# Layer 0 of a four-layer network: the up product of a group of rows in seven block products, relu and square on ScalarE, and two buffers for drawn weights

## The chip, the cores and the metric

The kernel runs on one core of a Trainium2 chip. The time is device microseconds of one execution of the whole program; the number given for a kernel is the median of its runs. Besides the timed runs there is one profiled execution, from which every duration below comes.

A core has five engines that the profile names: PE (TensorE, the matrix array), DVE (VectorE), ACT (ScalarE), POOL (GpSimd) and SP (SyncE, which here mainly issues DMAs). PEld is PE's loading of the stationary operand. They run their own instruction streams in order and wait for each other by semaphores. SBUF is the on-chip memory; PSUM takes the results of PE; this kernel uses it as eight banks of 128 by 512 float32.

## The reference

Four layers follow each other on x, 64 sequences of 32 rows, 512 wide (2048 rows in all), all in float32. Only layer 0 matters here:

```
w = weight[ids]                            # one of 8 drawn 512x512 matrices per sequence
y = einsum('bsi,boi->bso', x, w)
logits = y @ gate_w                        # 8 experts; the sum of the two largest is r
h = relu(y @ up_w) ** 2                    # 512 -> 1024
shared_out = h @ down_w                    # 1024 -> 512
routed_out = (((y @ fc1_w) @ expert_w) * r) @ fc2_w
x = x + layernorm(shared_out + routed_out) * gamma + beta
```

`y` and the product `y @ up_w` are the parts that the change touches. Layers 1 to 3 (layer 1 gated with low-rank adapters, layer 2 attention with a cache, layer 3 a drawn small product, each with a feed-forward part) stay as they are.

## The kernel before, in words

**Tiling.** `layer0` (L133) cuts the 2048 rows into 16 tiles of 128 rows, and the tiles into 4 groups of 4 tiles (N = 512 rows). A tile holds 4 sequences. Feature dimensions are cut into chunks of 128: 4 for the width 512, 8 for the 1024 features.

**The drawn product.** All 8 matrices lie in SBUF (`sets`). One `step` (L204 to L214) makes a quarter of one tile's `y`: it copies, for each of the 4 sequences of the tile, the drawn 128x512 block (an address read from a register) into `w`, the first `by` of them on DVE and the others on ACT (L208), and then issues 4 matmuls (L212), each with 32 rows of x as the stationary operand and one block as the moving one. They write four different groups of 32 rows of one bank, and the trace shows them beside each other. `w` comes from the pool `sp` with 3 buffers, handed out in turn: the copies of a step wait until PE has read the buffer that it takes over.

**Order of the work.** `on_pe` chains every matmul of the layer to the one issued before it, so PE runs in the order in which the program lists them. The other engines' orders are set by a scheduler, which keeps each engine's instructions in order of need.

1. Opening phase: 32 steps form `y` of groups 0 and 1 in 8 banks (k outermost, then 8 tiles), with `by` 3 and 2 in turn. `y` is then copied out of PSUM (`copied`, L242, and `second`, L253) and transposed (`turned`, L216 to L221: four PE transposes and an ACT copy into `yT`).
2. Group 0: for each of 8 chunks f, `features` (L266) makes 512 rows of one chunk: 4 matmuls of 128x512 into one bank `ph` (L225), ACT's relu from it into `hT` (L273), and DVE's multiplication of that with `ph` again (L274), which is relu squared. Beside the first four, `latent_rows` (L258) forms fc1 · expert.
3. Then tile after tile, in `Tile`: `choose` (the router and the latent product `pl`, top-2 sum, `routed`), `shared` in two halves (8 matmuls of `down` into `pd`), `turn` (two transposes into `eT`), `last` (fc2 on top of `pd`, then layernorm: DVE statistics, a power on POOL, DVE's `z` at L315, POOL's multiplication with gamma at L316 and addition of beta at L317, DVE's final addition at L318, and the store).
4. The steps for groups 2 and 3 (`products`, 16 per group, all 4 copies on DVE) are mixed as stretches into the features loops of groups 1 and 2: after each of the 7 remaining chunks 2 or 3 steps. Their `y` is transposed in the tile loop. The first chunk of the next group's features comes ahead of the last tile's `last`.

**PSUM.** Banks by tag: `tr` twice (transposes, `pl`, `latent_rows`), `mm` twice (`ph`, `pd`), and `y0` to `y3` for the four accumulators of `products`. The opening phase uses all eight for its eight tiles.

**Loads.** SP issues the loads in program order: ids; per k the x of groups 0 and 1 and the 8 blocks of `sets`; `up` in 8 pieces; `fc1T` and `expert`; gate; `down`; fc2; gamma and beta.

Of the kernel before, what the change touches and what calls it, by code (L numbers as in the profile page):

```python
# [36 lines left out]
SEQ = P // S  # L37
KC = D // P
# [94 lines left out]
def layer0(c, x_in, x_out):  # L133
# [4 lines left out]
    tc, nc, a = c.tc, c.nc, c.a  # L138
    INT, LAT, NE = 1024, 256, 8
    G = 4  # L140
    N = G * P
    n_sets = a["cond0T"].shape[0]
    with ExitStack() as ctx:

        fp = ctx.enter_context(tc.tile_pool(name="l0_first", bufs=1))
        sp = ctx.enter_context(tc.tile_pool(name="l0_seq_weights", bufs=3))
        tx = ctx.enter_context(tc.tile_pool(name="l0_transposed_x", bufs=2))
        up_p = ctx.enter_context(tc.tile_pool(name="l0_up", bufs=1))
        wp = ctx.enter_context(tc.tile_pool(name="l0_weights", bufs=1))
# [46 lines left out]
        def sets_of(g, *engines):  # L196

            _, ids = nc.values_load_multi_w_load_instructions(
                numbers[0:1, SEQ * G * g:SEQ * G * (g + 1)], engines=engines,
                min_val=0, max_val=n_sets - 1,  # L200
                skip_runtime_bounds_check_because="numbers holds them between the bounds")
            return ids

        def step(py, xT, ids, t, k, by):  # L204

            w = sp.tile([P, SEQ, D], F32, name="w")
            for j in range(SEQ):
                (nc.vector.tensor_copy if j < by else nc.scalar.copy)(  # L208
                    w[:, j, :], sets[:, k, ds(ids[SEQ * t + j], 1), :].rearrange("p a o -> p (a o)"))
            for j in range(SEQ):  # L210
                q = slice(S * j, S * j + S)
                c.on_pe(nc.tensor.matmul(  # L212
                    py[q, :], xT[:, k, t * P + S * j:t * P + S * j + S], w[:, j, :],
                    start=k == 0, stop=k == KC - 1))  # L214

        def turned(yT, t, y):  # L216

            pt = ps.tile([P, KC, P], F32, tag="tr", name="transposed")
            for k in range(KC):
                c.on_pe(nc.tensor.transpose(pt[:, k, :], y[:, k * P:(k + 1) * P], c.ident))  # L220
            nc.scalar.copy(yT[:, :, t * P:(t + 1) * P], pt)  # L221

        def part(out, pairs, first, last):
            for i, (lhsT, rhs) in enumerate(pairs):
                c.on_pe(nc.tensor.matmul(out, lhsT, rhs, start=first and i == 0,  # L225
                                         stop=last and i == len(pairs) - 1))

        def accumulators():
            return [ps.tile([P, D], F32, tag=f"y{t}", bufs=1, name="py") for t in range(G)]

        def products(g, xT):

            ids, pys = sets_of(g, mybir.EngineType.DVE), accumulators()
            for k in range(KC):
                for t in range(G):
                    step(pys[t], xT, ids, t, k, SEQ)
                    yield pys

        def copied(py, t):

            y = tp.tile([P, D], F32, name="y")
            (nc.scalar.copy if t % 2 else nc.vector.tensor_copy)(y, py)  # L242
            return y

        ids = [sets_of(g, mybir.EngineType.DVE, mybir.EngineType.Activation) for g in range(2)]
        pys = accumulators() + [ps.tile([P, D], F32, tag=("tr", "mm")[t // 2], name="py") for t in range(G)]
        for k in range(KC):
            for t in range(2 * G):
                step(pys[t], xTs[t // G], ids[t // G], t % G, k, 3 - t % 2)
        yTs = [gp.tile([P, KC, N], F32, name="yT") for _ in range(2)]  # L250
        second = gp.tile([P, INT // P, N], F32, name="second", tag="hT", bufs=1)
        for n in range(G):
            (nc.vector.tensor_copy if n % 2 else nc.scalar.copy)(second[:, n, :], pys[G + n])  # L253
        for t in range(G):
            turned(yTs[0], t, copied(pys[t], t))
        for t in range(G):
            turned(yTs[1], t, second[:, t, :])

        def latent_rows(m):
            pl = ps.tile([P, LAT], F32, tag="tr", name="pfe")  # L260
            part(pl, [(fc1T[:, k, m * P:(m + 1) * P], expert[:, k, :]) for k in range(LAT // P)], True, True)
            nc.scalar.copy(latent[:, m, :LAT], pl)

        hTs = {}

        def features(g, f):  # L266

            if f == 0:
                hTs[g] = gp.tile([P, INT // P, N], F32, name="hT", tag="hT", bufs=1)
            ph = ps.tile([P, N], F32, tag="mm", name="ph")  # L270
            part(ph, [(up[:, k, f * P:(f + 1) * P], yTs[g][:, k, :]) for k in range(KC)], True, True)
            h = hTs[g][:, f, :]
            nc.scalar.activation(h, ph, AF.Relu)  # L273
            nc.vector.tensor_tensor(h, h, ph, ALU.mult)  # L274

        class Tile:
            def __init__(self, T):
                self.T, self.g = T, T // G
                self.q = slice(T % G * P, (T % G + 1) * P)

            def choose(self):
                self.xt = c.load(xp, "xt", [P, D], x_in(self.T))
                pl = ps.tile([P, LAT + NE], F32, tag="tr", name="pl")
                part(pl, [(yTs[self.g][:, k, self.q], latent[:, k, :]) for k in range(KC)], True, True)
                top = tp.tile([P, 8], F32, name="top")
                nc.vector.max(top, pl[:, LAT:])
                r = tp.tile([P, 1], F32, name="routed_by")
                nc.vector.tensor_tensor(r, top[:, 0:1], top[:, 1:2], ALU.add)
                self.routed = tp.tile([P, LAT], F32, name="routed")
                nc.scalar.activation(self.routed, pl[:, :LAT], AF.Copy, scale=r)  # L290

            def shared(self, fs):
                if 0 in fs:
                    self.pd = ps.tile([P, D], F32, tag="mm", name="pd")
# [31 lines left out]
        done = {0: KC}  # L326
        for g in range(groups):
            xT = transposed_x(g + 1, None) if 0 < g < groups - 1 else None
            more = iter(()) if xT is None else products(g + 1, xT)
            for f in range(done.get(g, 0), INT // P):  # L330
                features(g, f)
                for _ in range(3 if f in (1, 4) else 2):
                    pys = next(more, None)
            tiles[G * g].choose()
            if xT is not None:
                yTs.append(gp.tile([P, KC, N], F32, name="yT"))
            for t in range(G):
                tile_ = tiles[G * g + t]
                tile_.shared(range(INT // P // 2))
                if xT is not None:  # L340
                    turned(yTs[g + 1], t, copied(pys[t], t))
                tile_.shared(range(INT // P // 2, INT // P))
# [1162 lines left out]
class Tail:  # L1505
# [3 lines left out]
    NE, R = 8, 16  # L1509
# [327 lines left out]
```

## Time and profile before

| | us |
|---|---|
| median of 3 runs | 3500.65 (3500.22 to 3505.04) |
| the profiled execution, its own time | 3498.47 |
| its span, first to last instruction | 3496.7 |
| granted PE clock, mean | 0.997 of full speed |
| layer 0 on PE, first to last matmul | 12.4 to 368.8 |
| opening phase on PE | 12.41 to 43.41 |
| first chunk of features | 49.54 |

| group of instructions of layer 0 | mean ns of one |
|---|---|
| L212 PE py, 128x32 by 128x512 | 613 |
| L225 PE ph, 128x128 by 128x512 | 597 |
| L208 DVE copy into w, 128x512 | 419 |
| L208 ACT copy into w, 128x512 | 617 |
| L273 ACT relu from PSUM, 128x512 | 598 |
| L274 DVE multiplication with PSUM, 128x512 | 687 |
| L303 ACT copy from PSUM, 128x256 | 373 |
| L318 DVE addition in SBUF, 128x512 | 691 |

A line of a group says: source line, engine, operation, result <- operands, shape, and count; then busy time with the mean of one, and the idle time just before with what ended it. A matmul's record is longer than its share of PE's time, since matmuls overlap: the share is read from starts of neighbours in the timeline. Each of these float32 matmuls has two records in the trace, which the text calls passes. In the windows, PEclk is the granted clock as a share of full speed, and DMA share the mean busy share of the 16 DMA engines.

### The profile page before, as it was taken

To read this page: it belongs to the slowest core of one execution; us is meant where nothing else is said; L and a number is where in the kernel's file an instruction comes from. 1 tells how busy PE (TensorE), PEld (TensorE's weight loads), DVE (VectorE), ACT (ScalarE), POOL (GpSimd) and SP (SyncE) were. 2 spreads that over 40 slices of the span, in tenths; PEclk is the share of its full clock that TensorE was granted. 3 is DMA by queue.
4 is the path that set the end of the run, shared out by engine and by line. 5 is a ranking of instruction groups with operands and counts; after the bars stand their busy time and mean duration, and the time that the engine had idled before them with its cause. 6 is when DMAs were issued, how large, how long until landed. Compare 5 with 4: busy or idle time off the path is not lost. (4 is left out here: it accounts for less than half of the span.)

```text
span 3496.7 us, 65764 instructions
## 1 busy us (share of the span) xinstructions
PE 3432.7 (98%) x20736; PEld 2601.2 (74%) x20736; DVE 2124.5 (61%) x5284; ACT 1554.7 (44%) x4089; POOL 1617.2 (46%) x1606
## 2 busy tenths in 40 slices
PE   8999999999999999999999999999999999999999
PEld 4445788888856778777787787777877778778755
DVE  4443534434457676766767767677676676766433
ACT  4111222222226555655555555555565555555411
POOL 0112432323336645645556455465564655644232
PEclk9999999999999999999999999999999999999999
DMA  6013454544466788888878888878888788887721
GB/s 220 25 34 126 159 168 154 168 151 157 139 202 213 239 261 251 259 258 256 257 249 258 255 250 258 262 251 267 256 260 262 247 267 250 259 259 241 228 85 58
DMA packets 630635, 736.00 MB, mean 210 GB/s; under 512 B 64274, under 2 KB 480018, under 8 KB 630290
## 3 DMA queue, kind: packets, MB, share of 16 engines
q1 hardware_dynamic: 577810, 558.74, 51.4%
q0 software_dynamic: 50176, 168.86, 13.9%
q8 instruction: 168, 2.75, 0.3%
q10 hardware_dynamic: 2304, 4.20, 0.3%
q14 instruction: 177, 1.45, 0.1%
HBM read 689.61 MB, written 41.94 MB: 209 GB/s over the span
## 5 line engine op out<-in xcount | busy, mean ns | idle before, releaser
L957 POOL DMA_INDIRECT vt<-in_v_rows,v_rows x512 | 512.5, 1001 | 304.9 <-PE po L931 178.7
L1220 ACT ACTIVATE pr<-pr,low 128x544 f32<-128x544 f32 x512 | 383.3, 749 | 532.3 <-DVE low L1218 486.0
L1213 PE MATMUL sc<-kt,qT 128*128 128x288 f32 (+1 forms) x2048 | 555.5, 394 | 8.1 <-DVE low L1218 6.5
L931 PE MATMUL po<-prT,vt 128*128 128x128 f32 x4096 | 544.9, 276 | 7.4 <-ACT prT L1231 5.9
L931 PEld LDWEIGHTS po<-prT,vt 128*128 128x128 f32 x4096 | 522.7, 192 | 39.1 <-ACT prT L1231 19.0
L1213 PEld LDWEIGHTS sc<-kt,qT 128*128 128x128 f32 x2048 | 385.1, 190 | 223.1 <-issue 123.0
L1218 DVE CUSTOM_DVE_ANT_0 pr<-sc,mask 128x544 f32<-128x544 f32 x512 | 368.2, 719 | 139.3 <-PE sc L1213 101.5
L1005 POOL TENSOR_TENSOR projected<-projected,swapped 128x512 f32<-128x512 f32 x160 | 208.4, 1302 | 300.9 <-DVE projected L1004 277.8
L1225 DVE TENSOR_SCALAR pr<-pr,low 128x512 f32<-128x512 f32 x512 | 315.3, 616 | 12.8
L926 PE MATMUL prT_ps<-ident,pr 128*128 128x128 f32 x2048 | 311.7, 275 | 2.6 <-DVE pr L1225 2.4
L1231 ACT COPY prT<-prT_ps 128x512 f32<-128x512 f32 x512 | 294.0, 574 | 35.2 <-PE prT_ps L926 20.1
L1222 DVE RECIPROCAL low<-low 128x1 f32<-128x1 f32 x512 | 82.0, 160 | 312.8 <-ACT pr L1220 245.7
L926 PEld LDWEIGHTS prT_ps<-ident,pr 128*128 128x128 f32 x2048 | 237.4, 142 | 11.8 <-issue 3.8
L931 PE MATMUL py<-wo,oT 128*128 128x256 f32 x1024 | 241.8, 379 | 0.0
L931 PE MATMUL pq<-wp,x_sums 128*128 128x512 f32 x512 | 240.8, 593 | 0.9 <-issue 0.5
L931 PEld LDWEIGHTS py<-wo,oT 128*128 128x128 f32 x1024 | 186.5, 190 | 21.1
L130 POOL TENSOR_TENSOR rs<-rs,minus_half 128x4 f32<-128x4 f32 x160 | 181.0, 1131 | 22.5 <-DVE low L1222 14.9
L931 PE MATMUL pq<-wp,xT 128*128 128x512 f32 x384 | 182.0, 597 | 3.9 <-DVE projected L1091 3.9
L931 PE MATMUL py<-wo,o_sum 128*128 128x256 f32 x768 | 181.4, 380 | 4.4 <-DVE o_sum L1149 2.5
L1223 ACT ACTIVATE own_pr<-pr,low 128x32 f32<-128x32 f32 x512 | 164.9, 322 | 46.2 <-DVE low L1222 37.4
L1006 POOL TENSOR_TENSOR projected<-projected,rs 128x512 f32<-128x512 f32 x160 | 172.4, 1078 | 7.9
L964 ACT COPY own_vt<-v 32x128 f32<-32x128 f32 x512 | 150.8, 295 | 54.9 <-PE po L931 42.4
(283 smaller groups left out, 6197.7 us busy)
## 6 DMA issues: line engine op xcount, KB each, us to landing
kt<-in_kT SPq DMA_DIRECT2D x2048, 64.0 KB
wp<-in_sums SPq DMA_DIRECT2D x192, 512.0 KB
wo<-out_sums SPq DMA_DIRECT2D x128, 512.0 KB
wp<-in_WqT SPq DMA_DIRECT2D x96, 512.0 KB
wo<-in_WoT SPq DMA_DIRECT2D x96, 512.0 KB
down1T<-in_down1T SPq DMA_DIRECT2D x80, 256.0 KB
wp<-in_WkT SPq DMA_DIRECT2D x32, 512.0 KB
xt<-x SPq DMA_DIRECT2D x48, 256.0 KB
```

The source lines that it names most:

```text
L130: self.nc.gpsimd.tensor_tensor(t, t, self.minus_half[:, :n], ALU.pow)
L926: c.on_pe(nc.tensor.transpose(pt[:, m, :], piece, c.ident))
L931: c.on_pe(nc.tensor.matmul(out, lhsT, rhs, start=first and i == 0, stop=last and i == len(pairs) - 1))
L957: nc.gpsimd.indirect_dma_start(out=vts[b % 2][:, n, :], out_offset=None, in_=a["v_rows"], in_offset=bass.IndirectOffsetOnAxis(ap=rows[h][: ...
L1005: nc.gpsimd.tensor_tensor(src, src, tmp, ALU.add)
L1006: nc.gpsimd.tensor_tensor(src, src, rs.unsqueeze(2).to_broadcast([P, REP, HD]), ALU.mult)
L1213: c.on_pe(nc.tensor.matmul(sc[:, lo + n * PSIZE:lo + m * PSIZE].rearrange("p (n k) -> p n k", k=PSIZE), q, kt[:, n:m, g, :], start=True, s ...
L1218: nc.vector.tensor_tensor_reduce(pr[:, :NK], sc[:, lo:lo + NK], masks[h, b], -SCALE, 3.0e38, ALU.add, ALU.min, low[:, 0:1])
L1220: nc.scalar.activation(pr[:, :NK], pr[:, :NK], AF.Exp, bias=low[:, 0:1], scale=-1.0, accum_out=low[:, 1:2])
L1223: nc.scalar.activation(own_prs[b % 2][:, g * S:(g + 1) * S], pr[:, L:NK], AF.Copy, scale=low[:, 2:3])
L1225: nc.vector.tensor_scalar(pr[:, :L], pr[:, :L], low[:, 2:3], None, ALU.mult)
L1231: last_prT.append(nc.scalar.copy(prT, pt).ins)
```

## The change

1. **The up product of a group.** yT (512 features by 512 rows) and `up` (512 by 1024) are treated as 2x2 blocks for each pair of chunks (f, f + 4): two halves of the contraction, two halves of the rows, and the two chunks. The class `Up` forms the four result blocks from seven block products (the Strassen-Winograd scheme) instead of eight; each product is 2 matmuls of 128x256 (`block`). The sums of `up` (`up_sums`, four DVE subtractions per pair) are made once, the sums of `yT` (`sums`, four DVE operations of 128x512) once per group. Three PSUM banks collect: a takes products 1, 6, 7; b takes 2 in its first half and 4 in its second; c takes 5 and 3. ACT copies the intermediate values v1, v5, v6, v7 out of PSUM, and four DVE additions make the result blocks in `hT`: L309 after product 2, L311 after 3, L314 after 7, L316 after 4.
2. **relu and square** are two ACT instructions for each chunk (L319, L320), on SBUF. DVE no longer multiplies.
3. **Order.** In group 0 the products run 1, 2, 5, 6, 3, 7, 4; in the others 1, 5, 6, 3, 7, 2, 4, with two steps of `products` after 5 and two after 7: eight stretches of two, where there were seven. Products 1 and 5 of the next group go ahead of the last tile's `last`.
4. **`products`** copies 3 blocks on DVE and 1 on ACT.
5. **Buffers.** `w` has two buffers instead of three. `fc1T` and `expert` are loaded into buffers of the tags `z` and `xt`. PSUM tags are single banks: tr, a, b, c, y0 to y3. `pl` goes to a, `pd` to c and b in turn, and the transposes after the opening phase alternate between tr and c.

The core of the diff:

```diff
-        sp = ctx.enter_context(tc.tile_pool(name="l0_seq_weights", bufs=3))
+        sp = ctx.enter_context(tc.tile_pool(name="l0_seq_weights", bufs=2))
...
-        ps = ctx.enter_context(tc.tile_pool(name="l0_psum", bufs=2, space=PSUM))
+        ps = ctx.enter_context(tc.tile_pool(name="l0_psum", bufs=1, space=PSUM))
...
-        fc1T = c.chunks(fp, "fc1T_0")
-        expert = c.chunks(fp, "expert0")
+        fc1T = [c.load(tp, "fc1T", [P, D], a["fc1T_0"][k * P:(k + 1) * P, :], tag="z") for k in range(LAT // P)]
+        expert = c.load(xp, "expert", [P, LAT // P, LAT], a["expert0"].rearrange("(k p) n -> p k n", p=P), tag="xt")
...
-                    step(pys[t], xT, ids, t, k, SEQ)
+                    step(pys[t], xT, ids, t, k, SEQ - 1)
...
+        def up_sums(f):
+
+            v11, v12, v21, v22, t1, t2, t3 = (v[:, :, f * P:(f + 1) * P] for v in
+                                              (b11, b12, b21, b22, t_up[:, 0], t_up[:, 1], t_up[:, 2]))
+            nc.vector.tensor_tensor(t1, v12, v11, ALU.subtract)
+            nc.vector.tensor_tensor(t3, v22, v12, ALU.subtract)
+            nc.vector.tensor_tensor(t2, v22, t1, ALU.subtract)
+            nc.vector.tensor_tensor(v12, v21, t2, ALU.subtract)
...
+                nc.vector.tensor_tensor(s1, x21, x22, ALU.add)
+                nc.vector.tensor_tensor(s2, s1, x11, ALU.subtract)
+                nc.vector.tensor_tensor(s3, x11, x21, ALU.subtract)
+                nc.vector.tensor_tensor(s4, x12, s2, ALU.subtract)
+                self.x = {1: x11, 2: x12, 3: s4, 4: x22, 5: s1, 6: s2, 7: s3}
...
+                out = {2: self.b[:, :H], 4: self.b[:, H:]}[m] if m in (2, 4) else self.c if m in (3, 5) else self.a
+                block(out, w, self.x[m], m in (1, 2, 5))
+                if m == 1:
+                    self.v1 = self.kept("v1", out)
+                elif m == 5:
+                    self.v5 = self.kept("v5", out)
+                elif m == 6:
+                    self.v6 = self.kept("v6", out)
+                elif m == 2:
+                    nc.vector.tensor_tensor(h[0][:, :H], out, self.v1, ALU.add)
+                elif m == 3:
+                    nc.vector.tensor_tensor(h[1][:, :H], out, self.v6, ALU.add)
+                elif m == 7:
+                    self.v7 = self.kept("v7", out)
+                    nc.vector.tensor_tensor(h[1][:, H:], out, self.v5, ALU.add)
+                elif m == 4:
+                    nc.vector.tensor_tensor(h[0][:, H:], out, self.v7, ALU.add)
+                if self.done % 7 == 0:
+                    for v in (h[1], h[0]):
+                        nc.scalar.activation(v, v, AF.Relu)
+                        nc.scalar.activation(v, v, AF.Square)
...
-            ph = ps.tile([P, N], F32, tag="mm", name="ph")
-            part(ph, [(up[:, k, f * P:(f + 1) * P], yTs[g][:, k, :]) for k in range(KC)], True, True)
-            h = hTs[g][:, f, :]
-            nc.scalar.activation(h, ph, AF.Relu)
-            nc.vector.tensor_tensor(h, h, ph, ALU.mult)
...
-        for m in range(KC):
-            features(0, m)
-            latent_rows(m)
+        first, order = (1, 2, 5, 6, 3, 7, 4), (1, 5, 6, 3, 7, 2, 4)
+        for f in range(FH):
+            if f + 1 < FH:
+                up_sums(f + 1)
+            for m in first:
+                ups[0].p(f, m)
+            latent_rows(f)
...
-            for f in range(done.get(g, 0), INT // P):
-                features(g, f)
-                for _ in range(3 if f in (1, 4) else 2):
-                    pys = next(more, None)
+            for i in range(ups[g].done, FH * 7):
+                if i % 7 in (2, 5):
+                    for _ in range(2):
+                        pys = next(more, None)
+                ups[g].p(i // 7, order[i % 7])
...
-                    features(g + 1, 0)
-                    done[g + 1] = 1
+                    for m in order[:2]:
+                        ups[g + 1].p(0, m)
```

Line numbers of added lines in the text are those of the changed kernel: the matmuls of the block products are L230, the sums of `up` L261 to L264, the sums of `yT` L276 to L279, the copies v L284.

More of the change, by code (lines that the diff above doesn't have):

```diff
@@ L214, in step, with turned @@
                     start=k == 0, stop=k == KC - 1))
-        def turned(yT, t, y):
-            pt = ps.tile([P, KC, P], F32, tag="tr", name="transposed")
+        def turned(yT, t, y, tag="tr"):
+            pt = ps.tile([P, KC, P], F32, tag=tag, name="transposed")
             for k in range(KC):
@@ L226, in part, with block @@
                                          stop=last and i == len(pairs) - 1))
+        def block(out, w, x, first):
+            for k in range(K2):
+                c.on_pe(nc.tensor.matmul(out, w[:, k, :], x[:, k, :], start=first and k == 0, stop=k == K2 - 1,
+                                         skip_group_check=not first))
         def accumulators():
-            return [ps.tile([P, D], F32, tag=f"y{t}", bufs=1, name="py") for t in range(G)]
+            return [ps.tile([P, D], F32, tag=f"y{t}", name="py") for t in range(G)]
         def products(g, xT):
-            ids, pys = sets_of(g, mybir.EngineType.DVE), accumulators()
+            ids = sets_of(g, mybir.EngineType.DVE, mybir.EngineType.Activation)
+            pys = accumulators()
             for k in range(KC):
                 for t in range(G):
-                    step(pys[t], xT, ids, t, k, SEQ)
+                    step(pys[t], xT, ids, t, k, SEQ - 1)
                     yield pys
@@ L243, in copied @@
             return y
+        K2, H, FH = KC // 2, N // 2, INT // P // 2
+        hTs = {}
+        b11, b12, b21, b22 = [up[:, k * K2:(k + 1) * K2, n * D:(n + 1) * D] for k in range(2) for n in range(2)]
+        t_up = up_p.tile([P, 3, K2, D], F32, name="up_sums")
+        blocks = {1: b11, 2: b21, 3: b22, 4: b12, 5: t_up[:, 0], 6: t_up[:, 1], 7: t_up[:, 2]}
+        def up_sums(f):
[5 more added lines that the diff above has]
+            nc.vector.tensor_tensor(v12, v21, t2, ALU.subtract)
@@ new lines, in layer0, with __init__, sums, kept @@
+        class Up:
+            def __init__(self, g):
+                self.g, self.done = g, 0
+            def sums(self):
+                x11, x12, x21, x22 = [yTs[self.g][:, k * K2:(k + 1) * K2, t * H:(t + 1) * H]
+                                      for t in range(2) for k in range(2)]
+                s = tx.tile([P, 4, K2, H], F32, name="y_sums", tag="xT")
+                s1, s2, s3, s4 = [s[:, i] for i in range(4)]
+                nc.vector.tensor_tensor(s1, x21, x22, ALU.add)
[3 more added lines that the diff above has]
+                self.x = {1: x11, 2: x12, 3: s4, 4: x22, 5: s1, 6: s2, 7: s3}
+            def kept(self, name, src):
+                t = tp.tile([P, H], F32, name=name, bufs=1)
+                nc.scalar.copy(t, src)
+                return t
+            def p(self, f, m):
+                if self.done == 0:
+                    hTs[self.g] = gp.tile([P, INT // P, N], F32, name="hT", tag="hT", bufs=1)
+                self.done += 1
+                h = [hTs[self.g][:, f + FH * n, :] for n in range(2)]
+                w = blocks[m][:, :, f * P:(f + 1) * P]
+                if m == 1:
+                    self.a = ps.tile([P, D], F32, tag="a", name="acc_a")[:, :H]
+                elif m == 2:
+                    self.b = ps.tile([P, D], F32, tag="b", name="acc_b")
+                elif m == 5:
+                    self.c = ps.tile([P, D], F32, tag="c", name="acc_c")[:, :H]
+                out = {2: self.b[:, :H], 4: self.b[:, H:]}[m] if m in (2, 4) else self.c if m in (3, 5) else self.a
+                block(out, w, self.x[m], m in (1, 2, 5))
+                if m == 1:
+                    self.v1 = self.kept("v1", out)
+                elif m == 5:
+                    self.v5 = self.kept("v5", out)
+                elif m == 6:
+                    self.v6 = self.kept("v6", out)
+                elif m == 2:
+                    nc.vector.tensor_tensor(h[0][:, :H], out, self.v1, ALU.add)
[10 more added lines that the diff above has]
+                        nc.scalar.activation(v, v, AF.Square)
@@ L245, in layer0 @@
         ids = [sets_of(g, mybir.EngineType.DVE, mybir.EngineType.Activation) for g in range(2)]
-        pys = accumulators() + [ps.tile([P, D], F32, tag=("tr", "mm")[t // 2], name="py") for t in range(G)]
+        pys = accumulators() + [ps.tile([P, D], F32, tag=("tr", "a", "b", "c")[t], name="py") for t in range(G)]
         for k in range(KC):
@@ L254, in layer0 @@
         for t in range(G):
-            turned(yTs[0], t, copied(pys[t], t))
+            turned(yTs[0], t, copied(pys[t], t), ("tr", "c")[t % 2])
+        ups = [Up(0)]
+        ups[0].sums()
+        up_sums(0)
         for t in range(G):
-            turned(yTs[1], t, second[:, t, :])
+            turned(yTs[1], t, second[:, t, :], ("tr", "c")[t % 2])
         def latent_rows(m):
             pl = ps.tile([P, LAT], F32, tag="tr", name="pfe")
-            part(pl, [(fc1T[:, k, m * P:(m + 1) * P], expert[:, k, :]) for k in range(LAT // P)], True, True)
+            part(pl, [(fc1T[k][:, m * P:(m + 1) * P], expert[:, k, :]) for k in range(LAT // P)], True, True)
             nc.scalar.copy(latent[:, m, :LAT], pl)
[L264 to L269, printed above, removed]
-            ph = ps.tile([P, N], F32, tag="mm", name="ph")
-            part(ph, [(up[:, k, f * P:(f + 1) * P], yTs[g][:, k, :]) for k in range(KC)], True, True)
-            h = hTs[g][:, f, :]
-            nc.scalar.activation(h, ph, AF.Relu)
-            nc.vector.tensor_tensor(h, h, ph, ALU.mult)
         class Tile:
@@ L282, in choose @@
                 self.xt = c.load(xp, "xt", [P, D], x_in(self.T))
-                pl = ps.tile([P, LAT + NE], F32, tag="tr", name="pl")
+                pl = ps.tile([P, LAT + NE], F32, tag="a", name="pl")
                 part(pl, [(yTs[self.g][:, k, self.q], latent[:, k, :]) for k in range(KC)], True, True)
@@ L293, in shared @@
                 if 0 in fs:
-                    self.pd = ps.tile([P, D], F32, tag="mm", name="pd")
+                    self.pd = ps.tile([P, D], F32, tag="cb"[self.T % 2], name="pd")
                 part(self.pd, [(hTs[self.g][:, f, self.q], down[:, f, :]) for f in fs], 0 in fs, False)
@@ L319, in last @@
                 nc.sync.dma_start(x_out(self.T), z)
-        for m in range(KC):
-            features(0, m)
-            latent_rows(m)
+        first, order = (1, 2, 5, 6, 3, 7, 4), (1, 5, 6, 3, 7, 2, 4)
[5 more added lines that the diff above has]
+            latent_rows(f)
         groups = NT // G
         tiles = [Tile(T) for T in range(NT)]
-        done = {0: KC}
         for g in range(groups):
@@ L341, in layer0 @@
                     turned(yTs[g + 1], t, copied(pys[t], t))
+                if t + 1 == G and g + 1 < groups:
+                    ups.append(Up(g + 1))
+                    ups[g + 1].sums()
                 tile_.shared(range(INT // P // 2, INT // P))
```

## The prediction, made before the change was run

> **What bounds the kernel now.** I read four views in this order: the busy table, the waits of TensorE (PE) inside layer 0, the windows, and PE's timeline. The page begins:
>
> ```profile
> span 3496.7 us, 65764 instructions
> PE 3432.7 (98%) x20736; PEld 2601.2 (74%) x20736; DVE 2124.5 (61%) x5284; ACT 1554.7 (44%) x4089; POOL 1617.2 (46%) x1606
> ```
>
> PE is busy for 98% of the span. A time is therefore the sum of what PE does, plus the holes in it. The view of waits for PE, restricted to layer 0 (0 to 370 us), says how few holes there are:
>
> ```profile
> PE py L212 <- DVE w L208: 12.4, 1, 12.4
> PE transposed L220 <- DVE y L242: 1.5, 1, 1.5
> PE pd L225 <- ACT eT L303: 0.5, 1, 0.5
> PE transposed L220 <- ACT yT L221: 0.4, 2, 0.2
> ```
>
> Columns: microseconds in all, number of waits, longest. Apart from the start (12.4) PE waits 2.4 us in 356. Whatever wait the change adds here goes straight into the time. The windows show the opening phase (the 32 steps that form y of groups 0 and 1):
>
> ```profile
> core 0: us, PE busy (x) PEld busy (x) DVE busy (x) ACT busy (x) POOL busy (x), PEclk, DMA share, GB/s
> 20.00:24.00 4.00, 4.00 (x43) 2.77 (x38) 3.98 (x12) 3.83 (x7) 0.00 (x0) 1.00 1.06 388
> 28.00:32.00 4.00, 4.00 (x42) 2.92 (x37) 4.00 (x13) 3.89 (x8) 0.00 (x0) 1.00 1.05 384
> 49.00:370.00 321.00, 319.31 (x1046) 148.62 (x1044) 139.44 (x341) 45.37 (x85) 57.51 (x50) 1.00 0.18 60
> ```
>
> The reader is to see that in this phase PE, VectorE (DVE) and ScalarE (ACT) are all full at once: three engines balanced on one pipeline of copied weights. From 49 us on only PE is full; DVE has more than half of its time free. So the two places must be judged apart. The timeline of PE gives the prices:
>
> ```profile
> 12.41 31.00 PE L212 MATMUL py<-w,xT 128*32 128x512 f32 x256 [12.41 <-DVE w L208]
> 49.54 3.60 PE L225 MATMUL ph<-yT,up 128*128 128x512 f32 x8
> 52.98 1.03 PE L225 MATMUL pfe<-expert,fc1T 128*128 128x256 f32 x4
> 53.84 3.60 PE L225 MATMUL ph<-yT,up 128*128 128x512 f32 x8
> 66.73 13.90 PE L225 MATMUL ph<-yT,up 128*128 128x512 f32 x32
> ...
> 132.47 3.70 PE L225 MATMUL ph<-yT,up 128*128 128x512 f32 x8
> 136.10 1.92 PE L212 MATMUL py<-w,xT 128*32 128x512 f32 x16
> 137.96 3.70 PE L225 MATMUL ph<-yT,up 128*128 128x512 f32 x8
> ```
>
> One feature chunk `ph` (8 records, 512 wide) takes 52.98 − 49.54 = 3.44 us, 3.433 over several, so 0.429 a record. The four 256-wide records of `pfe` take 53.84 − 52.98 = 0.86, so 0.2155 each: half the width costs half. A stretch of two steps takes 137.96 − 136.10 = 1.86 us.
>
> **What is removed.** Two chunks cost 2 × 3.433 = 6.87 us before. Seven block products are 28 records of 256 columns: 7 × 0.862 = 6.03. That is 0.83 us per pair; 4 groups of 4 pairs give **−13.3 us** if PE runs on without holes. Bounds: −13.3, and 0 if a lone product costs more than `pfe` shows. I take −13.3, since `pfe` is the same shape. From the end of the opening phase (43.41) to the first chunk (49.54) stand 6.13 us, with the 1.5 us wait for `y`. In the new order the copies of `y` stand further forward in the queues of DVE and ACT, and the transposes have a second bank as before: bounds 0 and −1.5, taken **−1.0**.
>
> **What is added: the opening phase.** `w` has two buffers instead of three. The first copy of a step waits for PE's last matmul of the step two before, and even and odd steps now keep one buffer each. So one buffer's loop bounds two steps. Its parts are these: three DVE copies, 2 × 0.336 + 0.42 = 1.10 us (or two ACT copies, 0.52 + 0.617 = 1.14); 0.054 from the end of a copy to its matmul; 0.429 for the first pass of that matmul; 0.592 for the last; 0.037 from the matmul's end to the next copy. All are single records of the trace. The sum is 2.21 to 2.25 us. Before, two steps took 1.717, which the third buffer made possible. The rows of these copies, 20 to 40 us:
>
> ```profile
> L208 DVE COPY w<-sets 128x512 f32 x58 | 20.0, 421 | 0.0
> L208 ACT COPY w<-sets 128x512 f32 x35 | 19.4, 617 | 0.6
> ```
>
> 58 copies in 20.0 us are one per 0.345 us without idle time; in the new loop DVE will sit idle. 16 × (2.25 − 1.717) = 8.5; the 0.87 us in which DVE reads the ids of group 1 (16.2 to 17.1 us) no longer has a spare buffer to cover it: **+9.4**. Bounds: 7.9 by the shorter loop without the ids, 10.5 with 2.35 us for copies that queue behind each other and two sums over `up` that now stand between them; and 0 if the loop is covered after all (first rival).
>
> One rule of the Trainium skill speaks against this edit more strongly. Row first: at 384 to 388 us PE is busy for only 1.60 and 1.34 of 2 us, and PEclk stays 1.00.
>
> ```profile
> 384.00:386.00 2.00, 1.60 (x15) 1.41 (x14) 1.00 (x3) 1.74 (x4) 1.33 (x2) 1.00 0.74 228
> 386.00:388.00 2.00, 1.34 (x13) 1.15 (x11) 1.81 (x5) 0.27 (x1) 1.73 (x3) 1.00 0.01 5
> ```
>
> The page "TensorE: Matmul & The Clock Gate", section "A second HAM failure mode: psum-queue depth-cycling", says that frequent short idle times of PE between groups of matmuls can throw the clock back and forth between half and full speed. At half speed throughout, by that rule, the phase would be bound by PE at 3.43 us for two steps and cost about 27 us instead of 9.4. Here PE would be idle for 0.5 us of every 2.2, which is about the share of the rows above, where the clock held. I keep 9.4 and leave a loss of clock to a rival.
>
> **What is added: group 0.** DVE forms the sums over `up` (16 subtractions of 128x256, 0.40 to 0.58 us each by the same subtractions of layer 1) and over `y` (4 of 128x512, 0.69 us each, per group). Most lie beside PE, but when the first pair's adds L311 and L314 fall due, DVE still has the sums of three later chunks and of group 1 ahead, and PE's next p1 waits for its bank: **+1.7** (0 to 3). The first `choose` waits for the last copy into `latent`, which ACT makes after four activations of 0.6 us: **+0.55** (0 to 1.2).
>
> **What is added: the waits in groups 1 to 3.** There is one more stretch per loop in groups 1 and 2. Group 1's loop took 166.24 − 126.23 = 40.0 us by the timeline; less 7 chunks (24.0) and 16 steps of 0.858 (13.7) that leaves 2.3 for the edges of seven stretches, 0.32 each; two more are **+0.64** (0.3 to 1). More important, the order p2, p4 puts two products of one bank next to each other: p4 writes the second half of bank b, and its first matmul waits for DVE's L309, which reads the first half. DVE can begin only when p2 is done. The nearest row is one wait of layer 1, where PE needs a bank that DVE must add from:
>
> ```profile
> 387.90 0.71 PE L450 MATMUL acc_a<-xT,up1T 128*128 128x128 f32 x4 [0.66 <-DVE up L587]
> ```
>
> 0.66 us with an add of 128 columns (0.279 us). An add of 256 columns I estimate at 0.42 from that row and L318's 0.69 for 512. So a bare stall is about 0.7: drain of p2, 0.42, and 0.055 to the matmul. Where three copies for the next stretch are ahead in DVE's queue it is 0.78, at the edges of a group 1.0 to 1.2. Behind p4 stands all of PE. In the first pair of a group DVE also still has `z` of the last tile, whose final add waits for POOL's multiply (1.28 us); behind it wait the copies of the second stretch (0.85 late) and, in group 3, L311 and L314. Group 1: 0.85 + 1.0 + 0.78 + 0.78 + 1.2 = 4.6. Group 2: 0.85 + 1.0 + 0.78 + 0.78 + 0.75 = 4.2. Group 3, without stretches: 0.25 at its first products, 1.9 for the first p4, 3 × 0.7 for the others, 0.3 until `pl` has bank a, 4.5. Together **+13.3** (bounds: 0 if DVE is through in time everywhere; 17 if each stall takes 1.2).
>
> **Costed at nothing.** relu and square: four ACT instructions of 0.6 per pair, against 6 to 9.5 us of PE per pair, and ACT was busy for 45 of 321 us. The four copies v (0.37 each) end before the next product ends that reads their bank. One copy of each step goes from DVE to ACT, one stretch ahead. `fc1T` and `expert` land in other buffers at the same time, before use. If ACT fell behind, p6 and p7 would wait 0.4 each. In group 2's tiles a cosine of a later layer now stands ahead of `eT` on ACT: 0 to 1.5 us, taken 0. Layers 1 to 3 keep their order; the first `xT_ps` still waits for the last `z`.
>
> **Sum.** −13.3 − 1.0 + 9.4 + 1.7 + 0.55 + 0.64 + 13.3 = +11.3. The profiled execution took 3498.47 us (span 3496.7), which gives 3509.8. The median of the runs, 3500.65, is 2.2 above it: **3512 us**.
>
> **Rivals.**
> 1. Two buffers are enough (the other side: not slower). Decides at a loop of 1.72 us per buffer, that is if matmuls of a step release the copies earlier or the copies run at 0.336 without the end. For it: DMA runs at 384 GB/s through the phase and `up` lands only by 38.6, so something else may have set it. Against it: `up` is there 11 us before use, and DVE is at 4.00 of 4. Price −9.4: 3502.5.
> 2. The stalls at p4 hide: DVE has 181 of 321 us free. But a stall is a chain and not a share. If they vanish, the time falls by about 10 (12 stalls): 3502.
> 3. Both: the products bring what they promise, 3512 − 9.4 − 10 = 3492.6, faster by 0.23%.
> 4. More waits than I count: PE's clock falls in the opening phase (it was half until 17.3 us in this trace, with records of 1.06 us for 0.61), or DVE's queue lets every stall reach 1.2 us, and the cosine falls due: +4 to +18, 3516 to 3530; I put 3522.
>
> That the products don't do what they say would be 28 records taking more than 6.87 us together; then only the losses remain, 3525, which I count into the fourth.
>
> **Chances.** Forecast 0.58 (its own range 3507 to 3517), rival 1 0.10, rival 2 0.13, rival 3 0.05, rival 4 0.14. A change under 0.2% (7 us: 3493.7 to 3507.7) is about what a measurement of this kernel can't tell from none. Faster 0.05 (rival 3); same 0.23 (rivals 1 and 2); slower 0.72. The range reaches from rivals 1 and 2 (3502, less 2 for the bounds of the smaller terms) to the lower part of rival 4: 3500 to 3520.
>
> **What would show it.** In the new profile PE's opening phase should end near 53 us with waits on copies L208 of about 0.5 per two steps, and DVE idle there; a phase end at 44 proves rival 1. Four 256-wide records should keep 0.86 us. The view of waits should name L309 as PE's releaser some 12 times at about 0.8; if it is absent, rival 2 holds. PEclk below 1.00 between 20 and 50 us would be rival 4. A shift after layer 0 would prove me wrong about the later layers.

## The result, and the profile after

The changed kernel took **3511.34 us** (median of 15 runs, 3506.12 to 3514.26). Beside it the kernel before took 3503.73 us (15 runs, 3497.21 to 3507.43). The ratio is 1.0024 with a 95% interval of 1.0016 to 1.0032: slower by 6 to 11 us. The profiled execution has a span of 3508.5 us, 11.8 above that of before. 3512 had been forecast from a first median of 3500.65; with more runs that median is 3503.73, so the closeness of the two absolute times is partly luck. The measured rise, 7.6 us between medians, is to be held against a forecast of +11.3.

The profile tells where. The stages of layer 0, from the starts of PE's records:

| stage of layer 0 (us) | before | changed | difference |
|---|---|---|---|
| start to the first up product | 49.54 | 56.24 | +6.70 |
| group 0, up product to its first `pl` | 30.92 | 27.63 | −3.29 |
| from there to the last tile's fc2 product | 286.38 | 292.73 | +6.35 |
| sum | 366.84 | 376.60 | +9.76 |

From layer 1 on the two traces stay 9.4 to 12.3 us apart. Those later 2 us are within what the later layers differ between single profiles (from layer 1's first product `low_ps` to the end, 3112 to 3127 us in the fourteen profiles of this study, except the one with a new wait at the start of layer 1), so only layer 0 is read to a microsecond.

The waits of PE in layer 0 of the changed kernel (microseconds in all, number, longest):

```profile
PE py L212 <- DVE w L208: 12.1, 1, 12.1
PE acc_b L230 <- DVE hT L309: 8.8, 12, 1.6
PE xT_ps L561 <- issue: 2.8, 1, 2.8
```

The second line is new: 12 waits at product 4, one for each pair of groups 1 to 3. But nothing in this view speaks of the opening phase, although it has become 7 us longer. Its windows, the line of PE's timeline, and three groups of 20 to 40 us:

```profile
20.00:24.00 4.00, 4.00 (x32) 1.40 (x26) 3.44 (x10) 3.25 (x6) 0.00 (x0) 1.00 1.05 387
28.00:32.00 4.00, 4.00 (x32) 1.44 (x29) 2.98 (x10) 3.12 (x6) 0.00 (x0) 1.00 1.05 384
```

```profile
12.05 38.43 PE L212 MATMUL py<-w,xT 128*32 128x512 f32 x256 [12.05 <-DVE w L208]
```

```profile
L208 DVE COPY w<-sets 128x512 f32 x45 | 15.9, 422 | 4.3 <-PE py L212 3.7 <-DMA sets<-in_cond0T 0.5
L208 ACT COPY w<-sets 128x512 f32 x27 | 15.9, 619 | 4.7 <-PE py L212 4.7
L212 PEld LDWEIGHTS py<-w,xT 128*32 128x32 f32 x141 | 7.4, 108 | 12.9 <-DVE w L208 12.2
```

PE is still "busy" for 4.00 of 4 us, since the matmuls of the four sequences overlap and a record counts as busy while it lasts. The count in brackets gives it away: 32 records instead of 42 or 43. So do DVE and ACT, which now sit idle for 4.3 and 4.7 of 20 us, 3.7 and 4.7 of that behind PE's release of a buffer, and PEld, which waits 12.2 us for DVE's copies. Each of them waits for another, in a loop through the two buffers. PEclk stays at 1.00.

Two stretches of the timeline show the second loss, in group 1 and in group 3:

```profile
145.32 1.92 PE L212 MATMUL py<-w,xT 128*32 128x512 f32 x16
147.18 1.13 PE L230 MATMUL acc_b<-yT,up 128*128 128x256 f32 x4
148.95 1.13 PE L230 MATMUL acc_b<-yT,up 128*128 128x256 f32 x4 [0.64 <-DVE hT L309]
149.92 1.03 PE L230 MATMUL acc_a<-yT,up 128*128 128x256 f32 x4
...
311.12 1.13 PE L230 MATMUL acc_b<-yT,up 128*128 128x256 f32 x4
313.86 1.13 PE L230 MATMUL acc_b<-yT,up 128*128 128x256 f32 x4 [1.61 <-DVE hT L309]
```

A product should take 0.86 us from start to start. Product 2 at 147.18 takes 1.77, that is 0.91 more: 0.64 in which PE is idle (in brackets), and the rest while its last records still run. Product 4 itself takes 0.97, 0.11 more than a product that follows another without a wait.

### The profile page after: what moved, and what is told of

Its sections match the earlier page's. It is cut to its first block, busy times and chain, and to the rows that moved or that the text cites. A ratio compares the mean times of both kernels' runs of the same rounds, so it can differ in the third digit from the quotient of the medians.

```text
span 3508.5 us, 66362 instructions
## 1 busy us (share of the span) xinstructions
PE 3436.3 (98%) x20928; PEld 2632.5 (75%) x20928; DVE 2135.6 (61%) x5316; ACT 1613.6 (46%) x4217; POOL 1614.7 (46%) x1606
## 5 line engine op out<-in xcount | busy, mean ns | idle before, releaser
L1306 ACT COPY prT<-prT_ps 128x512 f32<-128x512 f32 x512 | 293.9, 574 | 36.9 <-PE prT_ps L1001 19.3
```

The lines of the kernel that those rows point to most:

```text
L1306: last_prT.append(nc.scalar.copy(prT, pt).ins)
```

## The experiments

The theory was: (1) the seven products bring what they promise; (2) two buffers make the opening phase a loop of copies, matmuls and release; (3) PE waits at product 4 for DVE's L309, which reads the other half of its bank. The main rivals: the sums over `up`, which stand among DVE's copies, hold the opening phase; and DVE is late anyway, so that product 4 is only where it shows. The labels e1 to e12 are the names by which the expectations call the runs.

Beside most experiments the kernel before took 3492.6 to 3493.4 us, 10 us less than beside the result, so they are compared by their ratio to it and by layer 0's stages. "Step" is a drawn step; two steps took 1.72 us before and take 2.28 us in the changed kernel, from step 5 to the end. The first steps of the phase come with the loads and shift it by up to 1.5 us between profiles of the same code.

**Two buffers alone, on the kernel before (e1).**

```diff
-        sp = ctx.enter_context(tc.tile_pool(name="l0_seq_weights", bufs=3))
+        sp = ctx.enter_context(tc.tile_pool(name="l0_seq_weights", bufs=2))
```

> The kernel before, with two buffers for w and nothing else changed. Theory (one buffer's loop of copies, matmuls and release bounds two steps): in the opening phase two steps take 2.28 us as in the changed kernel, where they took 1.72; the last step starts near 49.9 instead of 42.8 us, and in groups 1 and 2 the stretches of three steps now wait for the third step's copies, 0.7 to 1.4 us at four places. The time rises by 8 to 13 us. Rival (the opening phase of the changed kernel is longer because of the sums over up that stand among DVE's copies): the opening phase stays at 1.72 for two steps and the time within 3 us.

3529.61 us, ratio 1.0106 (1.0089 to 1.0123): a rise of 36 us, some three times what was expected. Two steps take 2.28 us, to the hundredth what the changed kernel shows and without any sum over `up`: that confirms (2) against its rival. Groups 1 to 3 lose another 5.5 us. The remaining 20 us lie in layer 1, and were in nobody's sum. Its first products wait for a load:

```profile
PE acc_a L450 <- DMA gate1T<-in_gate1T: 8.1, 1, 8.1
PE acc_c L450 <- DVE sums_gate_up L724: 6.7, 1, 6.7
PE acc_a L450 <- DVE up L587: 5.6, 4, 3.8
```

The load of `gate1T` was issued at 325.7 us in the kernel before; here it is issued at 384.4, three microseconds ahead of its need, after SP's queue had waited at a load (L87) for PE's `pd` of the last tile (380 to 400 us):

```profile
SPq L87 <- PE pd L225: 4.5, 1, 4.5
```

The granted clock is low there as well: PEclk is 0.70 from 380 to 420 us, where the kernel before has 0.91 from 370 to 410. The three waits add up to 20.4 us; what the clock adds isn't separated.

**The same, with every other tile left where it was (e5).**

```diff
+        pad_p = ctx.enter_context(tc.tile_pool(name="l0_pad", bufs=1))
+        nc.gpsimd.memset(pad_p.tile([P, SEQ, D], F32, name="pad")[:, 0, :1], 0.0)
```

> The kernel before with two buffers for w, and the room of the third kept by an unused tile, so that every other tile lies where it lay. The first run of two buffers lost 10.8 us up to layer 1's first products and another 20 us there, where PE waited for DMA of gate1T. Theory (freeing the third buffer moved the later tiles, and layer 1's first weights came to lie where layer 0 reads until late): layer 0 still loses about 11 us, the 20 us go, and the time rises by 10 to 13 us. Rival (the loss in layer 1 comes from layer 0's longer run itself): the time rises by over 25 us again.

3506.8 us, ratio 1.0045 (1.0029 to 1.006), layer 0 12.2 us longer, and none of the three waits above. The rise is 14.2 us between medians, a little over the 10 to 13 expected. `gate1T` is issued at 338.0 us, and PEclk from 380 to 420 us is 0.91 again. So the 20 us came from the place of the tiles: with 8 KB a partition less in layer 0's pools, layer 1's first weights had to wait for memory that layer 0 reads to its end. The changed kernel doesn't show this wait (its `gate1T` is issued at 335.5 us); that its new tiles fill the freed room is the likely reason, and wasn't tried by itself.

**Product 4 in a bank of its own (e2).**

```diff
+                elif m == 4:
+                    self.d = ps.tile([P, D], F32, tag="tr", name="acc_d")
...
-                block(out, w, self.x[m], m in (1, 2, 5))
+                block(out, w, self.x[m], m in (1, 2, 4, 5))
```

> The changed kernel, with product 4 in a bank of its own (tr) instead of the second half of product 2's bank. Theory (PE waits at product 4 only because DVE's L309 reads the other half of the bank): the 12 waits for L309 go, each worth 0.7 to 1.9 us from start to start with the refilling of PE's pipeline, so 11 to 13 us less. Rival (DVE is late anyway, and the wait only names the first place at which PE meets it): PE waits for L309 or L316 at the next product that takes bank b, or for L314 at bank a, and the gain stays under 4 us.

Ratio 1.0009 (0.9999 to 1.0018). The 12 waits for L309 are gone. The stage from group 0's `pl` to the end takes 281.00 us instead of 292.73: 11.7 less, as expected. Group 0 loses 3.1 us, because `latent_rows` takes its turn in the same bank and waits for the addition of product 4:

```profile
62.80 1.03 PE L230 MATMUL acc_d<-yT,up 128*128 128x256 f32 x4
64.35 1.13 PE L225 MATMUL pfe<-expert,fc1T 128*128 128x256 f32 x4 [0.52 <-DVE hT L318]
```

**The same in groups 1 to 3 only (e6)** (`tag="tr"` where `self.g`, else the second half of b).

> The changed kernel with product 4 in the bank tr in groups 1 to 3 only. With tr in all groups the three later groups gained 11.1 us, and group 0 lost 3.1, since latent_rows uses tr and waited for the add of product 4. Theory: the 11 us stay and the 3.1 go: 10 to 12 us less than the changed kernel, that is layer 1's first products within 2 us of the kernel before. Rival (the loss of group 0 has another cause, a later add of L316): under 9 us less.

3492.36 us, ratio 1.0000 (0.9991 to 1.0009): level with the kernel before. Group 0 has its 27.63 us back, and the stage behind it takes 281.61. That is 11.1 us less than the changed kernel, and in the groups no new wait above 0.4 us took the place of those removed:

```profile
147.26 1.13 PE L230 MATMUL acc_b<-yT,up 128*128 128x256 f32 x4
148.22 1.03 PE L230 MATMUL acc_d<-yT,up 128*128 128x256 f32 x4
149.09 1.03 PE L230 MATMUL acc_a<-yT,up 128*128 128x256 f32 x4
```

So DVE was in time for all else. (3) holds and its rival falls.

**Another order instead of another bank (e3).**

```diff
-        first, order = (1, 2, 5, 6, 3, 7, 4), (1, 5, 6, 3, 7, 2, 4)
+        first, order = (1, 2, 5, 6, 3, 7, 4), (1, 5, 6, 3, 2, 7, 4)
```

> The changed kernel with the order 1, 5, 6, 3, 2, 7, 4 in groups 1 to 3, so that product 7 (and the second stretch) stand between 2 and 4. Theory: a stretch of 1.85 us or a product of 0.86 covers the 0.7 to 0.9 us that L309 needs; the waits at product 4 go except the first of group 3, of whose 1.9 us some 1.0 stays; in group 1 and 2 the late second stretch (1.1 us each) stays. 9 to 12 us less. Rival (DVE is late anyway): PE then waits for L309 or L314 behind the stretch, and the gain stays under 4 us.

A miss: ratio 1.0017 (1.0008 to 1.0027); the stage takes 288.23, only 4.5 us less, half of what was expected. The waits at product 4 shrink to one of 0.4, but others take their place. Products 7 and 4 now stand next to each other, so the next pair's product 1 waits a little for L314 (0.22 us a pair): groups 1 and 2 gain 2.9 and 2.4 us where their waits at product 4 had cost 4.3 and 3.4. Group 3, which has no stretches, loses 0.8. In its first pair product 2 comes earlier and waits 1.0 us for `z` of the last tile, whose `pd` has bank b. In the others relu and square of a pair (four ACT instructions, 2.4 us) start later, and ACT's copy v1 of the next pair stands behind them; product 6 waits for that copy:

```profile
316.96 1.13 PE L230 MATMUL acc_a<-yT,up 128*128 128x256 f32 x4
317.93 1.03 PE L230 MATMUL acc_c<-y_sums,up_sums 128*128 128x256 f32 x4
319.44 1.13 PE L230 MATMUL acc_a<-y_sums,up_sums 128*128 128x256 f32 x4 [0.48 <-ACT v L284]
```

So the rival was half right: not DVE but the queues behind the additions are tight, and an order that relieves one wait loads the next.

**A third buffer in the opening phase alone (e4).**

```diff
-            w = sp.tile([P, SEQ, D], F32, name="w")
+            w = (gp.tile([P, SEQ, D], F32, name="w", tag="hT", bufs=1) if third else
+                 sp.tile([P, SEQ, D], F32, name="w"))
...
+                n = 2 * G * k + t
+                step(pys[t], xTs[t // G], ids[t // G], t % G, k, 3 - t % 2, n % 3 == 2)
```

> The changed kernel with a third buffer for w in the opening phase alone (every third step takes it from the room of hT, which is free until then). Theory: two steps take 1.72 us again, the last step starts at 42.5 to 43.5 instead of 49.9 us, and the time falls by 6 to 7.5 us. Rival (the sums over up among the copies, or the copies' split, hold the phase): two steps stay above 2.1 us, and the time falls by under 2.

Ratio 1.0017 (1.0007 to 1.0027). Layer 0 is 4.2 us shorter than in the changed kernel, between the two forecasts, and both were partly right. Two steps take 1.72 us, but only up to the 24th step. Then there is a hole:

```profile
29.45 6.60 PE L213 MATMUL py<-w,xT 128*32 128x512 f32 x56
37.52 8.54 PE L213 MATMUL py<-w,xT 128*32 128x512 f32 x64 [1.47 <-DVE w L209]
```

```profile
L262 DVE TENSOR_TENSOR up_sums<-up 128x256 f32<-128x256 f32 x1 | 0.4, 424 | 2.2 <-DMA fc1T<-in_fc1T 2.2
```

The scheduler had put the first sum over `up` among the copies, and now the phase gets there before `up` has landed. DVE stands still for 2.2 us, and every copy behind it.

**The same, with the sums queued behind the phase (e7).** `last_copy` is the phase's last copy out of PSUM; the sums of the later pairs are queued in the same way.

```diff
+        with tc.issue_after(last_copy.ins):
+            up_sums(0)
```

> The changed kernel with the third buffer in the opening phase, and the sums over up queued on DVE behind the phase's last copy out of PSUM. In the third-buffer run alone two steps took 1.72 us until 34.6 us, and then one gap of 2 us and slower steps followed, ahead of which DVE had a sum that reads up, which had only just landed. Theory (DVE's queue stood behind that sum): the phase keeps 1.72 throughout, the last step starts at 42.5 to 43.2 us; DVE then has 5.4 us of sums after the phase, of which 0 to 3 reach PE in group 0. In all 4.5 to 7.5 us less than the changed kernel. Rival (DMA traffic or the missing id read is what slows the end of the phase): the gap near 34 to 38 us stays.

3494.31 us, ratio 1.0002 (0.9993 to 1.0012). The phase keeps 1.72 us, with no hole:

```profile
11.53 30.54 PE L213 MATMUL py<-w,xT 128*32 128x512 f32 x256 [11.53 <-DVE w L209]
```

30.54 us against 38.43. The first up product starts at 48.53 instead of 56.24; group 0 pays 1.0 us for the sums that DVE has left; layer 0 is 7.1 us shorter than in the changed kernel.

**The third buffer with the sums on POOL (e8)** (`nc.gpsimd.tensor_tensor` in `up_sums`, in their old place in the program).

> The same third buffer, with the sums over up on POOL instead of DVE. Theory: as with the sums queued behind the phase, the phase keeps 1.72 for two steps, and DVE is free after it; 5.5 to 7.5 us less than the changed kernel. A subtraction of 128x256 on POOL should take some 0.7 us (1.28 for 128x512), so the 16 are done by 50 to 52 us, when product 5 of the first pair needs the first four. Rival (POOL and DVE slow each other when both work in SBUF): DVE's copies take over 0.45 us each while POOL works, and the end of the phase comes later than 44 us.

Ratio 1.0028 (1.0017 to 1.004): of the 7.1 us that the run before this one gained in layer 0, 1.4 are left. Once POOL begins, at 36.9 us, two steps take up to 4.35 us. Groups of DVE and of POOL, 37 to 47 us:

```profile
L209 DVE COPY w<-sets 128x512 f32 x12 | 9.5, 860 | 0.0
L332 DVE COPY second<-py 128x512 f32<-128x512 f32 x1 | 0.7, 678 | 0.0
```

```profile
L262 POOL TENSOR_TENSOR up_sums<-up 128x256 f32<-128x256 f32 x4 | 3.6, 918 | 35.5 <-DMA fc1T<-in_fc1T 35.5
```

The rival holds; more under the last heading.

**Quarters of a buffer, no third one (e9)** (eight tiles of one sequence in the memory of the two buffers, sums behind the phase).

```diff
-            w = sp.tile([P, SEQ, D], F32, name="w")
+            w = [sp.tile([P, D], F32, name="w") for _ in range(SEQ)]
```

> The changed kernel with the memory of its two buffers for w handed out as eight quarters of one sequence each, so that a copy waits only for its own matmul of two steps before; the sums over up are queued behind the phase as in e7. No third buffer. Theory (the loop of a whole buffer, three copies in a row, is what costs; a quarter's loop is 0.42 + 0.05 + 0.43 + 0.59 + 0.04 = 1.53 us, under 1.72): two steps take 1.72 to 1.9 us, the last step starts before 44.5 us, and the time falls by 5 to 8 us against the changed kernel, nearly what the third buffer brought. Rival (what counts is how many steps the copies run ahead, and quarters run ahead no further): two steps stay above 2.1 us, less than 2.5 us gained.

Ratio 1.0015 (1.0006 to 1.0025). Two steps take 1.76 to 1.94 us until step 26, mostly 1.80 to 1.86, and 2.05 to 2.75 over the last few, where copies out of PSUM stand in the same queues. The first up product starts at 53.09 us, 3.1 earlier than in the changed kernel; group 0 and the groups behind it give back 0.6 and 1.0. In all layer 0 is 1.5 us shorter; 5 to 8 were expected, and the rival said under 2.5 with two steps above 2.1. The 1.0 goes with a fall of the granted clock, which no other run shows there: behind the wait for L309 in group 3's first pair (1.60 us, as in the changed kernel) PEclk is 0.57 from 311 to 315 us, and three products take 1.36, 1.70 and 1.32 us, 4.38 in all, where the changed kernel takes 2.69 with PEclk at 1.00. So in the loop itself smaller pieces in the same memory bring most of the way from 2.28 to 1.72 (some 1.83); but they are no full substitute for the room.

**Both remedies together (e10)** (third buffer, sums behind the phase, tr for product 4 in groups 1 to 3).

> The changed kernel with the third buffer in the opening phase, the sums over up behind the phase, and product 4 in the bank tr in groups 1 to 3. Theory (the two losses are independent): the gains add, 7.1 + 10.2 = 17 us below the changed kernel, with layer 1's first products some 7 us earlier than in the kernel before: 0.2% faster than it (ratio 0.997 to 0.999). Rival (a wait moves: group 0's sums on DVE, or the stretches, take part of it back): no more than 12 us below the changed kernel, that is within 0.05% of the kernel before.

**3484.29 us, ratio 0.9975 (0.9966 to 0.9985)**: faster than the kernel before by 0.25%. Layer 0 ends 17.0 us earlier than in the changed kernel and 7.2 earlier than before. The gains add: the three stages take 49.10, 28.58 and 281.95 us, each within 0.6 of the run that has the remedy or its side effect (48.53 and 28.60 in e7, 281.61 in e6). The seven products save 13.2 us, and not all of it reaches the time: against the kernel before, group 0 gains 2.3 of its 3.3 and the stage behind it 4.4 of 9.9 (the opening 0.4). The late second stretch of groups 1 and 2 (1.08 and 1.03 us) is still there.

**The same with quarters for the third buffer (e11).**

> As e10, but with quarters of w instead of the third buffer. Theory: the same gain in the opening phase if quarters hold 1.72 there, and in groups 1 and 2 the second stretch of the first pair, which stands behind z on DVE, starts with its ACT copies and single DVE copies earlier: 0 to 1 us less than e10. Rival: the phase stays slow, and it is 5 to 7 us above e10.

3488.61 us, ratio 0.9987 (0.9978 to 0.9996). Neither forecast came: layer 0 is 3.3 us longer than in e10, and all of it in the opening; the stage behind group 0 takes 281.99, so quarters bring nothing there.

**The changed kernel once more (e12).**

> The changed kernel itself once more, beside the kernel before on the chip of the experiments, on which the kernel before takes some 3493 us instead of 3504. Theory (the differences all lie in layer 0, whose stages repeat to 0.5 us): layer 1's first products again 9.3 to 10.3 us later than in the kernel before, and a ratio of 1.002 to 1.0035. Rival (part of the difference sits in the later layers and depends on the chip): a ratio outside 1.0016 to 1.004.

3512.03 us beside 3502.68, ratio 1.0028 (1.0017 to 1.0039). The kernel before took 10 us more than beside the other experiments, so this run doesn't say how the change stands where they ran. Layer 0 ended 10.8 us later than before, half a microsecond above the range given; its first up product started at 57.57 us instead of 56.24 (0.5 of that in the first four steps, 0.8 behind the start of the last step), while group 0 took the same 27.63 and the rest 292.47.

## Why the prediction was right

| term | forecast | measured in layer 0 |
|---|---|---|
| seven products for eight | −13.3 | −13.2 |
| opening phase with two buffers | +9.4 | +7.4 |
| from the phase to the first product | −1.0 | −0.4 |
| group 0, first pair | +1.7 | 0 |
| `choose` waits for `latent` | +0.55 | +0.60 |
| one more stretch in two groups | +0.64 | +0.8 |
| waits in groups 1 to 3 | +13.3 | +14.8 |
| sum | +11.3 | +9.8 |

(The terms measured are differences of starts in the trace. The phase also began 0.4 us earlier; with that they add up to the sum within 0.2.)

**The products.** Group 0 shows them pure: 28 products and four `pfe` at 0.863 us each, no hole, 3.29 us less than before: 4 × 0.82.

**The opening phase.** The mechanism and the loop were right: 2.28 us against 2.21 to 2.25 forecast. The size was off in two places, so that +7.4 lies below the 7.9 that was the least for a loop that shows. The first four steps take 6.06 us with three buffers and with two, so the loop costs 14 and not 16 times: 14 × 0.56 = 7.8, less 0.3 for two pairs of steps that took longer than 1.72 us before (1.81 and 1.94). And the 0.87 us of reading ids cost nothing that shows: they lie within these first steps. (The upper bound doesn't follow from its 2.35 us either: 16 × 0.633 is 10.1, or 11.0 with the ids, and not 10.5.) PE's records stayed at 0.59 to 0.62 us from the fifth step on, and PEclk at 1.00. (In the first step the records are 1.06 us long although PEclk reads 1.00 there too, so PEclk alone doesn't show a slow start.) The page "TensorE: Matmul & The Clock Gate" of the Trainium skill describes, in its section on psum-queue depth-cycling, a clock that oscillates with short idle times. For it the prediction put PE idle for 0.5 us of every 2.2; by its records PE was never idle here (4.00 of 4 us, with fewer records at once). So this phase doesn't test the rule.

**The first pair of group 0.** This step failed: the +1.7 was 0. It took the subtractions at 0.40 to 0.58 us, from records of layer 1. In the trace their record is 0.42 but the next begins after 0.335, and some were done during the phase. The queue was there (L314 stood half a microsecond behind a sum over `y` and a copy), but L314 ended at 62.5 us, ahead of the next p1 at 63.15. For a queue the distance between starts counts, 0.335 here, and not the 0.42 of the record.

**The waits at product 4.** Forecast 1.0, 0.78, 0.78, 1.2 in group 1, measured (start to start) 0.83, 0.91, 0.91, 1.65; group 2: 1.0, 0.78, 0.78, 0.75 against 0.84, 0.91, 0.91, 0.78; group 3: 1.9 and three of 0.7 against 1.88 and three of 0.68. What the sum lacked is mainly 0.11 at each of the 12 restarts of PE, 1.3 of the 1.5 in the table. (The figures start to start hold another 0.11 of a stretch's edge in groups 1 and 2; the table counts that with the stretches.) The late second stretch cost 1.07 and 1.04 where 0.85 was put.

The misses in the opening phase (−2.0) and in group 0's first pair (−1.7) and the one in the groups (+1.5) have opposite signs, so the sum is closer than its terms: that part is luck. Rivals 1, 2 and 3 are each what a run showed after a mend: with the third buffer (e7) layer 0 is 2.7 us above that of before, with the separate bank (e6) 0.5 below, with both 7.2 below. None of these was true of the change as made. Rival 4's slower clock did not come between 20 and 50 us. The second rival was right that DVE has time enough, and wrong that a share of idle time hides a chain.

## What to carry to other kernels

Fewer multiplications paid here only once the buffers and banks that the new scheme takes over were no longer those that kept another loop full: price the loop of one buffer (fill, use, release) against the busiest engine, before giving a buffer away. A product that takes over half of a bank while another engine still has to read the other half cost PE 0.7 to 1.9 us here, each time; put it into another bank, or put work of PE between the two, and then see which engine's queue the work that it delays stands in. And the size of one layer's pool can decide where the next layer's first loads lie and thus when they may start (20 us in e1).

## What the runs showed of the hardware

DVE and POOL slow each other when both work in SBUF. DVE's copy of 128x512 takes 0.42 us, and one started every 0.335; while POOL subtracts it took 0.94 to 0.96, one every 0.87, in step with POOL's subtractions (0.90 each, one every 0.87). DVE's copies out of PSUM kept their 0.68. The page "SBUF — State Buffer" of the Trainium skill, section "SBUF: two separate sides", says that the two engines share a pair of ports as an exclusive lock for a whole instruction, not as a share of bandwidth. The trace agrees: each of these copies ends 0.28 or 0.29 us after one of POOL's subtractions has ended, and a copy of 0.42 becomes one of 0.95. The one subtraction that ran beside copies out of PSUM alone took 0.73.

Not expected either: PE's busy time hides a slower rate when the matmuls of a step overlap (4.00 of 4 us at three quarters of the rate); the number of records and the waits of PEld show it.

And the granted clock can fall behind one short wait. In e9 PE was busy for 1.40 of 3 us from 308 to 311 us, and PEclk was 0.57 over the next four; in the changed kernel the same wait (1.61 us) left it at 1.00. The runs show no threshold.
